# First batch of a cross-attention and MoE kernel: its transposes, its statistics, and the order of the weights around it

## The chip, the cores and the metric

The kernel runs on one core of a Trainium2 chip, as one program. The metric is the time of one execution on the device in microseconds (us), median of several runs.

## The reference, cut to what matters

Four batches of 512 rows by 512 columns in float32 pass through two blocks.

```
# block 1, cross-attention that mixes columns            x: [4, 512, 512]
ln     = layernorm(x)                                     # eps 1e-5
query  = ctx @ Wq.T + bq ; key = ctx @ Wk.T + bk          # ctx [4,512,256] -> [4,512,128]
att    = softmax(query @ key.T)                           # [512, 512] of each batch
x1     = x + ln @ att.T

# block 2, transformer layer on h = layernorm(x1); result is x1 + block2(h)
a      = rmsnorm(h, ln1_w)
q,k,v  = a @ wq, a @ wk, a @ wv                           # 16 heads of 128, causal softmax
h      = h + attention(q, k, v) @ wo
m      = rmsnorm(h, ln2_w)
out    = h + (6 best of 16 experts, I = 352, weighted)(m) + shared_expert(m)   # SI = 704
```

## The kernel before, in words

**Precision.** Every float32 operand of a product is kept as two float16 tiles, a high and a low half. `split` makes them: ACT writes the high half (line 73, scaled and rounded), DVE the low half (line 74, the scaled source less the high half). `mm3` (lines 80 to 88) does every product in three passes: high by high (L83), high by low (L86) and low by high (L87).

**Transposes.** `flip` (L90) is a DMA transpose that SP issues. It turns the softmax of block 1 (`pn` into `ptp`), the normalised rows of block 1 (`hh` into `hT`) and the softmax of every attention head (`pn` into `pt`).

**Order.** The instructions of each engine are put in order by a scheduler from the order in which the program issues them, and `after(ins, first)` (L93) adds a dependence for the order alone. The dictionary `zz` holds the instructions that later ones are tied to. Weights are staged through tiles of the pool `stg`, which has two buffers.

**Block 1 of a batch** is the generator `xattn(b)` (from L203). It yields between small steps, and `step(b, n)` (L371) advances it by n of them. Its steps are:

- load of the context, its split into `ctp`, the products `xq` that make query and key (L275 to 287), and for batch 0 the split of the loaded x transposed into `lnp` (`turn`, L268: high half on ACT, low half on GpSimd, L273). One yield.
- four times, for 128 rows of the attention: the product `en` (L306), maximum on DVE, exponential on ACT, reciprocal, split into `pn`, transpose into `ptp`. Batch 0 yields once for each of these, the others twice.
- the statistics of x (`stats`, L249: four times `bn_stats` and `bn_aggr` on DVE, a power on GpSimd, and `nb` on DVE) and the centring of x by `nb` (`center`, L265, four instructions on GpSimd). Batch 0 does them behind its last softmax, the others between softmax steps.
- four times, for 128 rows of x: the product `xm` of 12 passes (L335), the residual on DVE, a DMA of the sum to `x1_d`, mean and variance on DVE, a power on GpSimd that makes `r2` (L346), `hu` on DVE, `hd` on GpSimd (L353, the value that the second block adds to), the split into `hh` (L360) and the transpose into `hT`. Three yields each.

Batch 0 is run whole (`step(0, 99)`, L375). Behind it come the load of `ln2b`, two zero rows that GpSimd writes, the gate's weights and their split. Then batch 1 is advanced by nine steps (L389), which are all of its energies. What is left of batch 1, twelve steps, is given out two at a time (L809) behind each of the first six heads. The main loop does the four heads of the first two groups of weights for batch 0 alone, and then each further group, which is two heads, for batch 0 and behind it for batch 1. So the first head of batch 1 is the seventh head of the main loop; before that head `step(b, 99)` (L762) finishes the batch.

**The main loop** (from L756) goes over heads. A head is `queries` (L613: two products of 512 columns by 12 passes, for the very first head in two halves of 256 columns), `values` for a new group (L599, in two halves), `project` of a group that is ready (L671), `scores` (L630: product, mask and maximum on DVE, exponential on ACT, split, transpose), and `attend` of the head before (L658). For the first head the first half of the values comes ahead of the first half of the queries, and these are the first uses of `hT`.

`fetch` (L406) brings a head's weights: for a first use a load by SP into a staging tile, `split` into the tile that the products read, and a DMA of both halves to a scratch in memory, from which later batches load. The first head's `wqk0` and `wv0` are loaded ahead of all that and split behind the last softmax step of batch 0 (`zz["calm"]`) and behind `nb`. The load of `wqk1` is tied to the last transpose of batch 0.

`warm` (L185) issues TensorE products whose results nobody uses: 10 at the start, 8 behind the first `xq`, 22 behind the last `en` of batch 0.

Of the kernel before, what the change touches and what calls it, by code (L numbers as in the profile page):

```python
# [17 lines left out]
P = 128  # L18
# [37 lines left out]
def xattn_moe_block_kernel(ctx: ExitStack, tc: tile.TileContext, x, xT, ctxT, wqkx, bqk, ln1, ln2,  # L56
# [18 lines left out]

    def split1(hi, lo, src, eng=nc.vector):
        return (nc.scalar.activation(hi, src, AF.Copy),
                eng.tensor_tensor(lo, src, hi, ALU.subtract))
# [11 lines left out]
    def flip(o, i):  # L90
        return nc.sync.dma_start_transpose(out=o, in_=i)

# [98 lines left out]

    warm(10)
# [10 lines left out]
    def xattn(b):  # L203
# [7 lines left out]
        if b == 0:  # L211
            xT32 = [turned(j) for j in range(2)]
        xt = (ap_ if b else x2p).tile([P, NT, D], F32, tag="xt" if b else "x2", name=f"xt{b}")
        nc.sync.dma_start(xt, x[b].rearrange("(t p) d -> p t d", p=P))
        if b == 0:
            nc.sync.dma_start(ln1b, ln1.partition_broadcast(P))
# [5 lines left out]
        for j, ins in enumerate(split(ctp[:, 0], ctp[:, 1], ct32, HS)):  # L222
            if b == 1:
                after(ins, zz["calm"][j])
# [24 lines left out]
        def stats():  # L249
            mv = asm.tile([P, NT, 2], F32, name="mvs", bufs=2)  # L250
            for m in range(NT):
                st = asm.tile([P, 6], F32, name="st")
                ins = nc.vector.bn_stats(st, xt[:, m, :])
                if b < 2:
                    after(ins, zz["hh", 0] if b else zz["sm", 0][1])
                nc.vector.bn_aggr(mv[:, m, :], st)
            ins = nc.vector.tensor_scalar(rs, mv[:, :, 1], 1e-5, PS * PS, ALU.add, ALU.mult)
            if b == 0:
                zz["calm"] = zz["sm", 0][0], ins
            nc.gpsimd.tensor_tensor(rs, rs, mhalf, ALU.pow)  # L260
            ins = nc.vector.scalar_tensor_tensor(nb, mv[:, :, 0], -PS, rs, ALU.mult, ALU.mult)
            if b == 0:
                zz["nb"] = ins

        def center(t):  # L265
            nc.gpsimd.tensor_scalar(xt[:, t, :], xt[:, t, :], nb[:, t:t + 1], None, ALU.add)
# [28 lines left out]
        for m in range(NT):  # L295
# [24 lines left out]
            zz["ptp", b] = flip(ptp[:, :, ml], pn)  # L320
            yield
        if b == 0:
            stats()
            after(nc.vector.tensor_scalar(ln1b, ln1b, HS, None, ALU.mult), zz["calm"][1])
            for t in range(NT):
                center(t)
            warm(22, last)
        if b < 2:
            x2s[b] = x2p.tile([P, NT, D], F32, tag="x2", name="x2")
        hT[b] = hpool.tile([P, 2 * C, S], F16, tag="hT", name=f"hT{b}")  # L330
        for t in range(NT):
            ps = bank("w", f"xm{b}_{t}")
            tl = slice(t * P, (t + 1) * P)
            xv = xt[:, t, :]
            zz["xm", b, t] = mm3(ps, [(lnp[:, c, tl], lnp[:, C + c, tl], ptp[:, c], ptp[:, C + c]) for c in range(C)])  # L335
            nc.vector.scalar_tensor_tensor(xv, ps, rs[:, t:t + 1], xv, ALU.mult, ALU.add)
# [23 lines left out]
            zz["hh", b] = split(hi, lo, hu, r2[:, 1:2])[1]  # L360
            zz["hT", b] = flip(hT[b][:, :, tl], hh)
# [13 lines left out]
    step(0, 99)  # L375
    ln2b = const.tile([P, D], F32, name="ln2b")
    nc.sync.dma_start(ln2b, ln2.partition_broadcast(P))
    after(nc.vector.tensor_scalar(ln2b, ln2b, HS, None, ALU.mult), zz["calm"][1])
    zrow = xp.tile([1, D], F32, tag="x1t", name="zrow", bufs=1)
# [885 lines left out]
```

## Time and profile before

| | |
|---|---|
| five runs, us | 1810.59, 1797.95, 1794.96, 1805.03, 1801.44 |
| their median, us | 1801.44 |
| the profiled execution, us | 1799.48 |
| its span, us | 1797.8 |
| mean granted TensorE clock | 0.983 |
| TensorE busy, us (share of the span) | 1727.1 (96%) |
| DVE busy, us | 1115.4 (62%) |
| ACT busy, us | 829.1 (46%) |
| GpSimd busy, us | 465.9 (26%) |

The profile is of one execution. Its span runs from the first to the last recorded instruction. PE is TensorE's products, PEld its weight loads, DVE is VectorE, ACT is ScalarE, POOL is GpSimd, and SP is the engine that issues most DMAs. Times are microseconds from the start of the span. In a row of the timeline come the start, the duration, the engine, the line of the program, the operation, the tiles written and read, their sizes, and in brackets how long the engine had waited and for whom. In a table of stages, each engine's busy time stands with the number of its instructions, and behind them the mean granted clock of TensorE (1.00 is full), the mean busy share of the 16 DMA engines and the GB/s that they moved.

### The profile page before, as it was taken

The numbers are of one execution on the slowest core, as the hardware profiler recorded it, in microseconds if no ns is written. First come the engines' busy times: TensorE is split into PE (matmuls) and PEld (weight loads), VectorE is DVE, ScalarE is ACT, GpSimd is POOL, SyncE is SP. The second block draws the span as 40 slices with busy tenths as digits, with TensorE's granted clock in tenths as the row PEclk, the third lists the DMA queues.
The fourth block names the chain that finished last, engine by engine and source line by source line (L and its number), as shares of the span: only waits on it lengthen the run. The fifth ranks groups of instructions, "written<-read, shape, count | busy, mean of one in ns | idle before, by whom it ended". The sixth has DMA issues, their size and how long they took to land. (4 is left out here: it accounts for less than half of the span.)

```text
span 1797.8 us, 27676 instructions
## 1 busy us (share of the span) xinstructions
PE 1727.1 (96%) x9919; PEld 933.9 (52%) x9919; DVE 1115.4 (62%) x2766; ACT 829.1 (46%) x1711; POOL 465.9 (26%) x576
## 2 busy tenths in 40 slices
PE   8899999999998999999999799999999999999998
PEld 3454555555554555556556344355555555555553
DVE  6786777777784677676667343744444444456755
ACT  4555655455543545554445322334444444444421
POOL 5423111130256252121113625300000000025653
PEclk9999999999998999999999899999999999999999
DMA  7876868475576776555457533755545545679766
GB/s 240 207 182 175 213 146 191 109 194 119 136 180 196 155 183 163 128 112 115 111 118 147 171 68 126 225 155 147 149 147 178 140 146 142 185 206 259 228 194 206
DMA packets 392724, 296.24 MB, mean 165 GB/s; under 512 B 334880, under 2 KB 335136, under 8 KB 391808
## 3 DMA queue, kind: packets, MB, share of 16 engines
q1 hardware_dynamic: 359456, 180.32, 42.6%
q0 software_dynamic: 33120, 114.06, 19.6%
q8 instruction: 80, 1.31, 0.3%
q14 instruction: 68, 0.56, 0.1%
HBM read 124.81 MB, written 88.94 MB: 119 GB/s over the span
## 5 line engine op out<-in xcount | busy, mean ns | idle before, releaser
L1140 POOL DMA_INDIRECT yg<-y_d,yrc x96 | 111.2, 1159 | 523.2 <-DVE hf L1043 441.1
L649 ACT ACTIVATE pe<-pe,bnm 128x128 f32<-128x128 f32 (+3 forms) x256 | 142.4, 557 | 161.9 <-DVE bnm L647 159.6
L83 PE MATMUL qk<-hT,wqk 128*128 128x512 f16 (+1 forms) x520 | 196.1, 377 | 6.3 <-DMA hT<-hh 6.3
L87 PE MATMUL qk<-hT,wqk 128*128 128x512 f16 (+1 forms) x520 | 196.0, 377 | 0.0
L86 PE MATMUL qk<-hT,wqk 128*128 128x512 f16 (+1 forms) x520 | 196.0, 377 | 0.0
L74 DVE SCALAR_TENSOR_TENSOR pn<-pe,brc,pn 128x128 f16<-128x128 f32 (+3 forms) x256 | 146.1, 581 | 22.4 <-ACT pn L73 16.9
L647 DVE CUSTOM_DVE_ANT_0 pe<-sc,causal 128x128 f32<-128x128 f32 (+3 forms) x256 | 117.2, 486 | 62.2 <-PE sc L644 54.8
L73 ACT ACTIVATE pn<-pe,brc 128x128 f16<-128x128 f32 (+3 forms) x256 | 133.7, 553 | 26.4 <-ACT pe L649 16.8
L86 PE MATMUL v<-wv,hT 128*128 128x256 f16 x512 | 140.4, 274 | 2.5 <-issue 2.4
L87 PE MATMUL v<-wv,hT 128*128 128x256 f16 x512 | 140.6, 275 | 1.8 <-issue 1.8
L83 PE MATMUL v<-wv,hT 128*128 128x256 f16 x512 | 140.2, 274 | 1.5 <-DMA hT<-hh 0.8
L83 PE MATMUL g<-xT,wt 128*128 128x384 f16 (+2 forms) x384 | 127.3, 331 | 0.0
L86 PE MATMUL g<-xT,wt 128*128 128x384 f16 (+2 forms) x384 | 127.2, 331 | 0.0
L87 PE MATMUL g<-xT,wt 128*128 128x384 f16 (+2 forms) x384 | 127.2, 331 | 0.0
L1029 ACT ACTIVATE hT_e<-hf 128x384 f16<-128x384 f32 (+3 forms) x96 | 51.0, 532 | 141.9 <-DVE hf L1043 133.7
L681 DVE SCALAR_TENSOR_TENSOR x<-wo,x 128x512 f32<-128x512 f32 x128 | 87.5, 687 | 37.2 <-PE wo L87 36.9
L83 PE MATMUL y<-dt,hT_e 128*128 128x512 f16 (+1 forms) x288 | 109.4, 380 | 0.0
L87 PE MATMUL y<-dt,hT_e 128*128 128x512 f16 (+1 forms) x288 | 108.9, 378 | 0.0
L86 PE MATMUL y<-dt,hT_e 128*128 128x512 f16 (+1 forms) x288 | 108.9, 378 | 0.0
L73 ACT ACTIVATE qkt<-qk 128x512 f16<-128x512 f32 x128 | 74.6, 586 | 71.9 <-PE qk L87 70.5
L463 POOL DMA_INDIRECT xs_d<-h2p,slotu x96 | 96.5, 1005 | 27.6 <-issue 27.5
L74 DVE SCALAR_TENSOR_TENSOR qkt<-qk,qkt 128x512 f16<-128x512 f32 x128 | 87.6, 687 | 21.7 <-ACT qkt L73 17.9
(323 smaller groups left out, 4034.9 us busy)
## 6 DMA issues: line engine op xcount, KB each, us to landing
y_d<-yt SPq DMA_DIRECT2D x96, 256.0 KB
est<-in_ew_dram SPq DMA_DIRECT2D x32, 704.0 KB
est<-in_ed_dram SPq DMA_DIRECT2D x16, 768.0 KB
wqk<-wqk_d POOLq DMA_DIRECT2D x20, 512.0 KB
wqk_st<-in_wqk_dram SPq DMA_DIRECT2D x16, 512.0 KB
wqk_d<-wqk POOLq DMA_DIRECT2D x15, 512.0 KB
xs_d<-causal POOLq DMA_DIRECT2D x16, 384.0 KB
wv<-wv_d POOLq DMA_DIRECT2D x10, 512.0 KB
```

The lines of the kernel that those rows point to most:

```text
L73: return (nc.scalar.activation(hi, src, AF.Copy, scale=scale), nc.vector.scalar_tensor_tensor(lo, src, scale, hi, ALU.mult, ALU.subtract))
L74: nc.vector.scalar_tensor_tensor(lo, src, scale, hi, ALU.mult, ALU.subtract))
L83: ins = nc.tensor.matmul(o, lh, rh, start=start and j == 0, stop=False)
L86: nc.tensor.matmul(o, lh, rl, start=False, stop=False)
L87: ins = nc.tensor.matmul(o, ll, rh, start=False, stop=stop and j == n - 1)
L463: ins = nc.gpsimd.indirect_dma_start(out=xs_d, out_offset=bass.IndirectOffsetOnAxis(ap=slotu[:, tt, k:k + 1], axis=0), in_=h2ps[tt], in_of ...
L647: nc.vector.tensor_tensor_reduce(pe, ps[:, :w], causal[:, S - w:], -1.0, 3e38, ALU.add, ALU.min, nm)
L649: nc.scalar.activation(pe, pe, AF.Exp, bias=nm, scale=-1.0, accum_out=sm)
L681: nc.vector.scalar_tensor_tensor(x2[:, t, :], ps, 1.0 / (VS * WS), x2[:, t, :], ALU.mult, ALU.add)
L1029: nc.scalar.activation(hT[:R, ic, :w], hf, AF.Copy)
L1140: nc.gpsimd.indirect_dma_start(out=yg, out_offset=None, in_=src, in_offset=bass.IndirectOffsetOnAxis(ap=idx[:, tt, k:k + 1], axis=0))
```

## The change

The program computes the same. For batch 0 of block 1 it differs in these points; batches 1 to 3 keep the DMA transposes and the statistics where they were.

- `swap` replaces `flip` for `ptp` and `hT` of batch 0: for each half, four products with an identity matrix in float16 (`id16`) put the transposed blocks into a PSUM bank, and a copy brings them to SBUF. The high halves' copies are on ACT, the low halves' on DVE (`ptp`), or all on ACT (`hT`).
- x of batch 0 is loaded ahead of its transposed form, which now follows behind it on SP.
- The statistics of batch 0 are tied behind the third of the four transposes. Its centring is on ACT instead of GpSimd.
- The last run of `warm` has 12 products instead of 22.
- `xm` of batch 0 is done in pieces: the first two row blocks by 128 columns, in the order in which `ptp` comes, the last two whole, in the banks of the tag `s`. The residual of the last two is tied behind the second `hh`.
- Batch 0 is advanced by 11 steps, which are its first two row blocks. Its remaining steps, and what stood behind them, are now in `second_half`, which is called in the first head between the first and the second halves of values and queries. `second_half` then advances batch 1 by five steps; the main loop by four instead of two behind each of the first six heads.
- `wqk1` is fetched ahead of `second_half`, and held for the second head.
- In the first six heads, `fetch` uses `split_in_place` instead of `split`: ACT writes the high half and then scales the staged weights in place, and GpSimd subtracts.

```diff
@@ -73,6 +73,13 @@
         return (nc.scalar.activation(hi, src, AF.Copy, scale=scale),
                 nc.vector.scalar_tensor_tensor(lo, src, scale, hi, ALU.mult, ALU.subtract))
 
+    def split_in_place(hi, lo, src, scale):
+        ins = nc.scalar.activation(hi, src, AF.Copy, scale=scale)
+        more = nc.scalar.activation(src, src, AF.Copy, scale=scale)
+        if "center" in zz:
+            after(more, zz["center"])
+        return ins, nc.gpsimd.tensor_tensor(lo, src, hi, ALU.subtract)
+
     def split1(hi, lo, src, eng=nc.vector):
         return (nc.scalar.activation(hi, src, AF.Copy),
                 eng.tensor_tensor(lo, src, hi, ALU.subtract))
@@ -89,6 +96,16 @@
 
     def flip(o, i):
         return nc.sync.dma_start_transpose(out=o, in_=i)
+
+    def swap(o, i, tag, low):
+        done = []
+        for a, put in enumerate((nc.scalar.copy, low)):
+            ps = bank(tag, "swap")
+            for c in range(C):
+                j = (a * C + c) * P
+                nc.tensor.matmul(ps[:, c * P:(c + 1) * P], i[:, j:j + P], id16, start=True, stop=True)
+            done.append(put(o[:, a * C:(a + 1) * C, :], ps.rearrange("p (c q) -> p c q", c=C)))
+        return done
 
     def after(ins, first):
         tc.add_manual_dep(ins.ins, first.ins.name,
@@ -189,6 +206,8 @@
             if first:
                 after(ins, first)
 
+    id16 = ap_.tile([P, P], F16, name="id16")
+    nc.vector.tensor_copy(id16, ident)
     warm(10)
     ct0 = ctx_load(0)
     wx32 = at_.tile([P, 2 * CC * P], F32, tag="f", name="wx32")
@@ -208,11 +227,10 @@
             nc.sync.dma_start(t, xT[b, j])
             return t
 
-        if b == 0:
-            xT32 = [turned(j) for j in range(2)]
         xt = (ap_ if b else x2p).tile([P, NT, D], F32, tag="xt" if b else "x2", name=f"xt{b}")
         nc.sync.dma_start(xt, x[b].rearrange("(t p) d -> p t d", p=P))
         if b == 0:
+            xT32 = [turned(j) for j in range(2)]
             nc.sync.dma_start(ln1b, ln1.partition_broadcast(P))
             for nm, src in (("wqk0", wqk[0]), ("wv0", wv[0])):
                 t = vp.tile([P, NT, 2, GW], F16, tag="vt", name=f"{nm}_st")
@@ -221,7 +239,7 @@
         ctp = ap_.tile([P, 2, CC, S], F16, tag="lnp", name="ctp")
         for j, ins in enumerate(split(ctp[:, 0], ctp[:, 1], ct32, HS)):
             if b == 1:
-                after(ins, zz["calm"][j])
+                after(ins, zz["hh", 0] if j else zz["hi", 0])
         spare = dict(pm=[(he, "pe3"), (xp, "h2"), (he, "pe3"), (xp, "x1t")],
                      pn=[(hq, "qk0"), (hq, "qk1"), (he, "pn3"), (rp, "h2p")], hh=[(he, "pn3"), (rp, "h2p")])
         spare.update(hu=spare["pm"], qf=spare["pm"])
@@ -252,17 +270,17 @@
                 st = asm.tile([P, 6], F32, name="st")
                 ins = nc.vector.bn_stats(st, xt[:, m, :])
                 if b < 2:
-                    after(ins, zz["hh", 0] if b else zz["sm", 0][1])
+                    after(ins, zz["hh", 0] if b else zz["third"])
                 nc.vector.bn_aggr(mv[:, m, :], st)
             ins = nc.vector.tensor_scalar(rs, mv[:, :, 1], 1e-5, PS * PS, ALU.add, ALU.mult)
+            nc.gpsimd.tensor_tensor(rs, rs, mhalf, ALU.pow)
+            zz["nb"] = nc.vector.scalar_tensor_tensor(nb, mv[:, :, 0], -PS, rs, ALU.mult, ALU.mult)
+
+        def center(t):
             if b == 0:
-                zz["calm"] = zz["sm", 0][0], ins
-            nc.gpsimd.tensor_tensor(rs, rs, mhalf, ALU.pow)
-            ins = nc.vector.scalar_tensor_tensor(nb, mv[:, :, 0], -PS, rs, ALU.mult, ALU.mult)
-            if b == 0:
-                zz["nb"] = ins
-
-        def center(t):
+                zz["center"] = nc.scalar.activation(xt[:, t, :], xt[:, t, :], AF.Identity, bias=nb[:, t:t + 1])
+                after(zz["center"], zz["calm"][0])
+                return
             nc.gpsimd.tensor_scalar(xt[:, t, :], xt[:, t, :], nb[:, t:t + 1], None, ALU.add)
 
         def turn(j, t):
@@ -317,23 +335,43 @@
             nc.vector.tensor_scalar(rc, rc, PS, None, ALU.mult)
             pn, hi, lo = pair(tmp("pn", F16))
             zz["sm", b] = split(hi, lo, pm, rc)
-            zz["ptp", b] = flip(ptp[:, :, ml], pn)
+            if b:
+                flip(ptp[:, :, ml], pn)
+            else:
+                zz["third"] = zz["calm"][1] if m else None
+                zz["calm"] = swap(ptp[:, :, ml], pn, "a", nc.vector.tensor_copy)
             yield
         if b == 0:
+            after(nc.vector.tensor_scalar(ln1b, ln1b, HS, None, ALU.mult), zz["calm"][1])
             stats()
-            after(nc.vector.tensor_scalar(ln1b, ln1b, HS, None, ALU.mult), zz["calm"][1])
             for t in range(NT):
                 center(t)
-            warm(22, last)
+            warm(12, last)
         if b < 2:
             x2s[b] = x2p.tile([P, NT, D], F32, tag="x2", name="x2")
         hT[b] = hpool.tile([P, 2 * C, S], F16, tag="hT", name=f"hT{b}")
+        def product(t, tag):
+            ps = bank(tag, f"xm{b}_{t}")
+            tl = slice(t * P, (t + 1) * P)
+            zz["xm", b, t] = mm3(ps, [(lnp[:, c, tl], lnp[:, C + c, tl], ptp[:, c], ptp[:, C + c]) for c in range(C)])
+            return ps
+
+        early_xm = [bank("w", f"xm{b}_{t}") for t in range(0 if b else 2)]
+        for m in range(NT):
+            ml = slice(m * P, (m + 1) * P)
+            for t, ps in enumerate(early_xm):
+                tl = slice(t * P, (t + 1) * P)
+                zz["xm", b, t] = mm3(ps[:, ml], [(lnp[:, c, tl], lnp[:, C + c, tl], ptp[:, c, ml], ptp[:, C + c, ml])
+                                                 for c in range(C)])
+        if b == 0:
+            early_xm += [product(t, "s") for t in range(2, NT)]
         for t in range(NT):
-            ps = bank("w", f"xm{b}_{t}")
             tl = slice(t * P, (t + 1) * P)
             xv = xt[:, t, :]
-            zz["xm", b, t] = mm3(ps, [(lnp[:, c, tl], lnp[:, C + c, tl], ptp[:, c], ptp[:, C + c]) for c in range(C)])
-            nc.vector.scalar_tensor_tensor(xv, ps, rs[:, t:t + 1], xv, ALU.mult, ALU.add)
+            ps = product(t, "w") if b else early_xm[t]
+            ins = nc.vector.scalar_tensor_tensor(xv, ps, rs[:, t:t + 1], xv, ALU.mult, ALU.add)
+            if b == 0 and t >= 2:
+                after(ins, zz["hh", 0])
             q = nc.gpsimd if b else nc.sync
             q.dma_start(x1_d[b][:, t, :], xv)
             st = asm.tile([P, 6], F32, name="st")
@@ -357,8 +395,11 @@
                 nc.sync.dma_start(out[b, tl], hd)
             yield
             hh, hi, lo = pair(tmp("hh", F16))
-            zz["hh", b] = split(hi, lo, hu, r2[:, 1:2])[1]
-            zz["hT", b] = flip(hT[b][:, :, tl], hh)
+            zz["hi", b], zz["hh", b] = split(hi, lo, hu, r2[:, 1:2])
+            if b:
+                flip(hT[b][:, :, tl], hh)
+            else:
+                swap(hT[b][:, :, tl], hh, "as"[t // 2], nc.scalar.copy)
             yield
 
     if stop == "A":
@@ -372,21 +413,24 @@
         for _ in range(n):
             next(bg[b], None)
 
-    step(0, 99)
+    step(0, 5 + 6)
     ln2b = const.tile([P, D], F32, name="ln2b")
-    nc.sync.dma_start(ln2b, ln2.partition_broadcast(P))
-    after(nc.vector.tensor_scalar(ln2b, ln2b, HS, None, ALU.mult), zz["calm"][1])
-    zrow = xp.tile([1, D], F32, tag="x1t", name="zrow", bufs=1)
-    nc.vector.memset(zrow, 0.0)
-    nc.gpsimd.dma_start(y_d[0:1, :], zrow)
-    nc.gpsimd.dma_start(yo_d[0:1, :], zrow)
     g32 = const.tile([P, C * E], F32, name="g32")
-    nc.sync.dma_start(g32, gate)
     gtp = const.tile([P, 2, C, E], F16, name="gtp")
     gtf = gtp.rearrange("p a c e -> p a (c e)")
-    for j, ins in enumerate(split(gtf[:, 0], gtf[:, 1], g32, WS)):
-        after(ins, zz["calm"][j])
-    step(1, 1 + 2 * NT)
+
+    def second_half():
+        step(0, 99)
+        nc.sync.dma_start(ln2b, ln2.partition_broadcast(P))
+        after(nc.vector.tensor_scalar(ln2b, ln2b, HS, None, ALU.mult), zz["hh", 0])
+        zrow = xp.tile([1, D], F32, tag="x1t", name="zrow", bufs=1)
+        nc.vector.memset(zrow, 0.0)
+        nc.gpsimd.dma_start(y_d[0:1, :], zrow)
+        nc.gpsimd.dma_start(yo_d[0:1, :], zrow)
+        nc.sync.dma_start(g32, gate)
+        for j, ins in enumerate(split(gtf[:, 0], gtf[:, 1], g32, WS)):
+            after(ins, zz["hh", 0] if j else zz["hi", 0])
+        step(1, 5)
 
     shx = {}
 
@@ -402,6 +446,7 @@
             pieces.append((sdw[:, :, j:j + 1024], sd[:, j:j + 1024]))
 
     held, partner, seen = {}, {}, set()
+    low_on_pool = [True]
 
     def fetch(b, g, pool, tag, n, src, scr, nm):
         if held.get(nm, (None,))[0] == (b, g):
@@ -418,17 +463,14 @@
             st_ = early_st[nm]
         else:
             st_ = stg.tile([P, 1024], F32, tag="st", name=f"{nm}_st")
-            ins = nc.sync.dma_start(st_[:, :n], src)
-            if nm == "wqk1":
-                after(ins, zz["hT", 0])
-        for j, ins in enumerate(split(w[:, 0], w[:, 1], st_[:, :n], WS)):
-            if first:
-                after(ins, zz["nb"] if j else zz["calm"][0])
+            nc.sync.dma_start(st_[:, :n], src)
+        cut = split_in_place if low_on_pool[0] else split
+        for j, ins in enumerate(cut(w[:, 0], w[:, 1], st_[:, :n], WS)):
+            if j == 0 and (first or nm == "wqk1"):
+                after(ins, zz["calm"][0] if first else zz["center"])
         ins = (nc.sync if nm == "wqk0" else nc.gpsimd).dma_start(scr, w.rearrange("p a n -> p (a n)"))
         if nm != "wqk0":
             zz["pad"] = ins
-        if nm == "wqk0":
-            after(ins, zz["ptp", 0])
         return w
 
     pieces = []
@@ -754,11 +796,13 @@
     ready = []
     bring = iter([j for j in range(2, B) for _ in range(5 * NT + 1)])
     for n in range(NH + LAG + 1):
+        low_on_pool[0] = n < 6
         if n < NH:
             b, h = heads[n]
             if b not in opened:
                 opened.add(b)
-                step(b, 99)
+                if n:
+                    step(b, 99)
                 if b == B - 1:
                     shared_pool()
             parts = [queries(b, h)]
@@ -768,6 +812,8 @@
                 parts.reverse()
                 for p in parts:
                     next(p)
+                held["wqk1"] = (0, 0), fetch(0, 0, wp, "wqk", 1024, wqk[1], wqk_d[1], "wqk1")
+                second_half()
             for p in parts:
                 for _ in p:
                     pass
@@ -806,7 +852,7 @@
         if H // 2 <= n < H // 2 + E:
             pad_rows(n - H // 2)
         if n < 6:
-            step(1, 2)
+            step(1, 4)
         else:
             for _, j in zip(range(2 - n % 2), bring):
                 step(j)
```

## The prediction

> **What bounds the kernel now.** I read the page first, then the stages of the opening, then TensorE's waits, then single rows of the timeline.
>
> The page:
> ```profile
> span 1797.8 us, 27676 instructions
> ...
> PE 1727.1 (96%) x9919; PEld 933.9 (52%) x9919; DVE 1115.4 (62%) x2766; ACT 829.1 (46%) x1711; POOL 465.9 (26%) x576
> ```
> TensorE is busy 96% of the span. A change that leaves its products alone can only shorten the time in which it does not stream. The changed program's order of products is the old one again, row for row, from about a quarter of the kernel on, so what counts is how much is lost before that.
>
> The stages up to 200 us (PE, PEld, DVE, ACT, POOL busy, then clock, DMA share, GB/s):
> ```profile
> 0.00:41.11 41.11, 32.14 (x124) 12.76 (x124) 28.57 (x71) 18.77 (x31) 20.36 (x23) 0.92 0.80 254
> 41.11:51.75 10.64, 7.36 (x58) 5.51 (x58) 8.86 (x17) 4.17 (x6) 9.15 (x6) 1.00 0.40 87
> 51.75:77.97 26.22, 20.62 (x136) 13.08 (x137) 18.46 (x45) 15.70 (x31) 11.16 (x12) 0.99 0.88 207
> 77.97:145.12 67.15, 62.88 (x359) 34.16 (x359) 57.57 (x167) 39.37 (x89) 12.80 (x17) 0.98 0.85 212
> ```
> TensorE's waits in the first 200 us, and the rows that end them:
> ```profile
> PE qk L83 <- DMA hT<-hh: 6.3, 2, 3.3
> PE sc L642 <- DVE bnm L647: 5.6, 1, 5.6
> PE xm L83 <- DMA ptp<-pn: 5.6, 1, 5.6
> ```
> ```profile
> 51.75 0.28 PE L83 MATMUL qk<-hT,wqk 128*128 128x256 f16 x1 [3.28 <-DMA hT<-hh]
> ...
> 73.52 0.72 ACT L73 ACTIVATE pn<-pm,rc 128x512 f16<-128x512 f32 x1 [4.78 <-DMA ptp<-pn]
> ...
> 77.97 0.37 PE L642 MATMUL sc<-qkt,qkt 128*128 128x256 f16 x1 [5.61 <-DVE bnm L647]
> ...
> 145.12 0.39 PE L83 MATMUL qk<-hT,wqk 128*128 128x512 f16 x1 [3.03 <-DMA hT<-hh]
> ```
> The stall before 77.97 goes back through DVE and ACT to a DMA transpose of batch 1. At 145.12 the first product of batch 1's heads waits for batch 1's last transpose. I take that product as the meeting point: before it both programs do the same products.
>
> **The yardstick.** From 57.65 to 60.67 fourteen products of 512 columns start, 0.2157 us each: one unit. Ahead of the meeting point lie xq 24, en 24, xm 96, six heads' queries 144, three groups' values 72, scores 45, five heads' av 37.5, two wo 48: 490.5 units, 105.8 us. Before loses 145.1 - 105.8 = 39.3 us, and 1.7 more in the half-clock window (3.41 us) after the stall: 41.0. On the way, at 41.11, 84 units (18.1) are done: 23.0 lost; at 51.75, 26.3; the third stall adds 5.6 and a half-clock window 1.7, the fourth 3.0, crumbs 2.7.
>
> **The change, part by part.**
>
> *TensorE transposes, first batch.* Eight DMA transposes go (SP issue 1.24 to 2.79 us each). 64 products of 128 columns come, 0.055 us apart in the score rows: 3.5 us, in gaps where TensorE waits anyway (uncovered, they would cost 3.5). Sixteen evictions come; no row has them, the nearest are the 0.58 (ACT) and 0.68 us (DVE) of the vt halves. The last softmax halves end at 18.15 (ACT) and 19.04 (DVE) as before. With three banks and two copies squeezed between, DVE's third copy ends near 21.5; the four moved statistics (2.47 us) stand ahead of the fourth in DVE's queue, which ends near 24.6. Before, the last transpose landed at 25.1: 0.5 us won.
>
> *Statistics, centring.* After 24.6: ln1b 0.42, aggregates 0.36, rs 0.17, GpSimd's power 1.16, nb 0.15, then centring on ACT 0.7: the first residual runs at 27.7 (30.24 before; centring left GpSimd, where four took 8.16 us). Two residuals and statistics at DVE's row prices give the first r2 at 30.9.
>
> *Low halves on GpSimd.* Its row for the same form, 2.13 us, replaces DVE's 1.22; ACT pays an in-place scaling, 1.05, for each. Eleven weights: DVE -13, GpSimd +23, ACT +12 us. Here it bites: ACT scales wv only behind four centrings, at 30.4. GpSimd's queue is then wv low (to 32.6), power (0.75, 33.3), wqk low (35.5), power (36.2). hh follows 0.72 on ACT, 0.74 on DVE, then transposes: the first v product at 38.0. With collisions on the SBUF port:
> ```profile
> 44.63 2.13 POOL L273 TENSOR_TENSOR lnp<-xT,lnp 128x1024 f16<-128x1024 f32 x1
> 44.69 2.08 DVE L351 SCALAR_TENSOR_TENSOR nb<-mv,r 128x1 f32<-128x1 f32 x1 [1.25 <-POOL r L346]
> ```
> a 0.15 us instruction took 2.08, until GpSimd's was done. Two of the hu and hh steps could each lose a us: 40.0. I take 38.5, for most small DVE steps beside GpSimd's earlier 2.13 us rows (13.90 on) kept their 0.15. By then 72 units are done (15.5 us; batch 1's xq is no longer there): 23.0 lost, as before.
>
> The Trainium skill, SBUF — State Buffer, section "SBUF: two separate sides", says that a DVE instruction with two SBUF inputs and a GpSimd instruction lock each other out for a whole instruction, which speaks against this part. By that rule the start would be 40.0 and the final sum 1.5 us later.
>
> *Second half of batch 0.* GpSimd after 36.2: a DMA issue (0.8), the second head's low half (39.1), two hd (0.76 and 1.78), an issue (0.6), third power 43.0; hh, residual and statistics again, fourth power near 47.5; hh, then ACT has batch 1's ctp (1.05) ahead of two copies: queries' second half at 50.3, against 51.75. But TensorE then has only v and q to do: 20.7 us done, 29.6 lost, 3.3 more than before, because xq and en of batch 1 (4.5 us) filled that gap. Idle through a whole clock window, it restarts at half clock: about 1.6, 31.2 lost.
>
> *Second head's weights early, third's late.* The order on SP puts the third head's load behind staging that GpSimd frees: power, four centrings (1.57 each), one low half of xT, 65.2 us. Load 3.9 (50.17 to 54.03), hi 1.05, an exp 0.7, scaling 1.05, low 2.13: 74. TensorE gets there near 71.7 to 72.5: 0 to 4 us, I take 1.5. The fourth head's load stands on SP ahead of three transposes for the first attend and waits for that low half: they issue from 74.3, the last lands near 80 if it takes 3.1 as at 37.92. TensorE arrives near 77.7: I take 2.4; with the row at 65.69, whose transpose landed after 13.5 us, it is 12.
>
> *Batch 1 in steps of four.* Its last xm moves ahead of the fifth head: the 3.0 us wait and 1.7 of half clock at 145 go. DVE, 57.57 of 67.15 us busy, is relieved: crumbs 1.7 for 2.7. xt's load ahead of xT moves xT back by xt's 2.8 us, to 11.1; ACT reads it at 11.6: nothing, but with 0.5 us to spare (beyond, ACT's softmax slips with it). Ten fewer warm-up products lie in idle time.
>
> *Sum.* 31.2 + 1.5 + 2.4 + 1.7 = 36.8 against 41.0: 4.2 us less. The profiled execution took 1799.5 us (span 1797.8 and 1.7 around it): 1795.3. The median of the five runs is 2.0 above it, so I forecast 1797.
>
> A rule on the clock bears on the attend stall. These stretches of one clock window show TensorE's busy time, clock and DMA:
> ```profile
> 1012.64:1016.05 3.41, 1.39 (x5) 1.00 0.95 278
> 1016.05:1019.46 3.41, 0.94 (x2) 0.50 0.37 151
> 186.61:190.02 3.41, 1.72 (x15) 1.00 0.77 240
> 190.02:193.43 3.41, 3.21 (x17) 1.00 0.91 287
> ```
> A window 1.39 busy was followed by half clock, one 1.72 busy was not. So a stall of 1.9 us can cost 1.7 more, and I keep that for the range. The skill's TensorE: Matmul & The Clock Gate, section "What's actually happening", asks for an idle window of about 3.4 us; by it the stall of 2.4 costs nothing further. The row differs, and it decides.
>
> **The rivals.** (About 0.5%, 9 us, is what a measurement of this kernel can tell from no change.)
>
> *Within 0.5%, forecast, 0.44.* Earlier start and a later wait nearly cancel.
>
> *Faster, 0.35.* GpSimd and SP keep up: start at 38.0, second half at 49 with 28.3 lost, no half clock, neither weight nor attend waits, crumbs 1.7: 30.0 lost, 11 us won, 1790. For it: the DMAs are spread out and eight transposes fewer are in the way. Against it: GpSimd's 2.13 us rows stand in one queue with the powers.
>
> *Slower, 0.21.* SP's order becomes the bound. If the first attend's last transpose takes 13.5 us as at 65.69, the wait is 12.7 instead of 2.4; with one half-clock window (1.7) and the xm transposes behind (1.3), 13 more: 1810. It decides from 13 us in flight on. For it: DMA share 0.88 at that place; against: the loads are now paced.
>
> The unknowns' ends give 1790 and 1810; the five runs lie 6.5 below and 9.2 above their median, and a median of runs moves by about half of that at most: 1783 to 1812. Faster 0.35, same 0.44, slower 0.21.
>
> **What would show it.** Right: no DMA transpose of ptp or hT for batch 0; first v product near 38.5, TensorE idle some 7 us before queries near 50; waits of 1 to 3 us before the third head's queries and the first av; no wait at batch 1's first queries; losses up to there near 37 us. Wrong: GpSimd's low half well off 2.1 us; v later than 40; an av wait over 10; a wait at the meeting point still; or the later three quarters of the kernel changing by more than a few us, which none of these steps explains.

## The result and the profile after

The changed kernel takes 1812.66 us (median of 44 runs), the kernel before 1808.12 (median of 86): ratio 1.0024, interval [1.0013, 1.0036], 4.3 us slower. The forecast, 1797, was 4.4 us below the median of the five runs that it started from, and that median lies 6.7 us below the one of all 86. The profiled execution took 1807.8 us.

The page, then the stages up to the point where the 105.8 us of products ahead of batch 1's first head are done (151.2; columns as before):

```profile
span 1806.1 us, 27928 instructions
...
PE 1730.2 (96%) x10045; PEld 941.1 (52%) x10045; DVE 1113.2 (62%) x2760; ACT 848.8 (47%) x1738; POOL 475.9 (26%) x583
```
```profile
0.00:41.12 41.12, 29.78 (x223) 16.65 (x224) 28.20 (x63) 26.09 (x40) 16.57 (x20) 0.92 0.54 199
41.12:51.78 10.66, 8.71 (x68) 6.62 (x66) 7.68 (x19) 5.22 (x10) 5.28 (x7) 0.82 0.47 148
51.78:84.75 32.97, 26.58 (x146) 14.27 (x144) 24.17 (x74) 25.31 (x53) 17.03 (x12) 0.95 0.46 121
84.75:151.20 66.45, 64.05 (x367) 35.44 (x368) 51.01 (x135) 38.92 (x75) 29.63 (x30) 0.97 0.90 225
```

The first v product starts at 41.12, where it started before (41.11). The 3.0 us wait at batch 1's first head is gone, the 5.6 us wait too. In their place, in TensorE's waits of the first 200 us, stand the transposes of hh, the scores and the first av (in each row: us in total, how many waits, the longest):

```profile
PE swap L106 <- ACT hh L73: 6.5, 3, 3.6
PE sc L684 <- ACT qkt L73: 4.0, 2, 2.1
PE av L90 <- DMA pt<-pn: 3.4, 1, 3.4
PE sc L684 <- DVE bnm L689: 2.3, 2, 2.0
...
PE sc L685 <- DVE qkt L74: 1.2, 1, 1.2
...
PE sc L684 <- ACT pm L332: 1.0, 2, 0.8
```

By the forecast's yardstick (time at which n us of products are done, less n; warm-up and transposes not counted), at 120 us of products, just behind the meeting point, the changed kernel has lost 45.3 us and the one before 41.1. At 200 us of products it is 53.2 against 45.4. These two marks (lost at 120 and at 200 us of products) and the start of the first v product ("first v") are given for every kernel below, each from its one profile.

### The profile page after: what moved, and what is told of

Same layout as the page of the kernel before. It is cut to its first block, busy times and chain, and to the rows that moved or that the text cites. A ratio compares the mean times of both kernels' runs of the same rounds, so it can differ in the third digit from the quotient of the medians.

```text
span 1806.1 us, 27928 instructions
## 1 busy us (share of the span) xinstructions
PE 1730.2 (96%) x10045; PEld 941.1 (52%) x10045; DVE 1113.2 (62%) x2760; ACT 848.8 (47%) x1738; POOL 475.9 (26%) x583
## 3 DMA queue, kind: packets, MB, share of 16 engines
q0 software_dynamic: 33120, 114.06, 19.2%
## 4 chain that ended last, share of the span: by engine, by line
PE 64%; DMA 6%; issue 5%; DVE 5%; ACT 1%; POOL 1%; another core or an unknown queue 1%; SPq 0%; POOLq 0%; ACTq 0%; DVEq 0%
PE qk L93 4%; PE qk L94 4%; PE qk L90 4%; PE g L93 3%; PE g L90 3%; PE g L94 3%; PE y L90 3%; PE y L93 3%; PE y L94 3%; DMA yg<-y_d,yrc 3%; PE wo L93 2%; PE wo L94 2%; PE wo L90 2%; PE u L90 2%; PE u L94 2%
## 5 line engine op out<-in xcount | busy, mean ns | idle before, releaser
L1186 POOL DMA_INDIRECT yg<-y_d,yrc x96 | 106.6, 1110 | 530.5 <-PE u L94 439.7
```

What stands on the lines that cost most here:

```text
L1186: nc.gpsimd.indirect_dma_start(out=yg, out_offset=None, in_=src, in_offset=bass.IndirectOffsetOnAxis(ap=idx[:, tt, k:k + 1], axis=0))
```

## The experiments

Three parts of the change could be undone alone. F: the low halves of the first three weights (wv0, wqk0, wqk1). L: those of the later weights of the first six heads. X: batch 1's xq, which before filled the gap between batch 0's two halves. The experiments were run in five sessions. In the first two (e1 to e8) the kernel before takes 1771 to 1772 us, in the other three 1797 to 1807. Ratios are to the kernel before in the same session, from 8 to 12 runs of each changed program. What separates the two kinds of session is not known: chip number 4 of the record gave 1771 us in one session and 1799 in a later one.

**Low halves on DVE.**
```diff
-        cut = split_in_place if low_on_pool[0] else split
+        cut = split
```


> The changed kernel with the low halves of all early weights on DVE again (split in place of split_in_place), nothing else changed. Theory A (GpSimd's low halves and ACT's extra scalings are what came out dearer than forecast): hu and nb of the first rows take 0.74 and 0.16 us again instead of 2.65 and 2.08, the first v product comes near 38.9 instead of 41.1, the staging tiles come free some 2 us earlier, so the wait before the first av falls from 3.4 to under 1 us without a half-clock window behind it; lost up to the first head of batch 1 about 38 instead of 45.4 us, time about 6 us below the changed kernel, ratio to before 0.999. Rival B (batch 1's energies, now among the first heads' scores, overfill DVE and ACT between 62 and 86 us, and DVE gets 1.22 us more for each weight): the start gains 2 us, the waits from 70 to 118 us stay or grow, time within 2 us of the changed kernel. Rival C (the swaps' round trips set the start): v stays at 41.

Ratio 0.9992 [0.9965, 1.0019]. First v 38.72; lost 41.7 at the first mark, 45.5 at the second. The start came as theory A said, the time too; less of the middle came back than it said (41.7, not 38).

**Only the later ones on DVE (L).**
```diff
-        low_on_pool[0] = n < 6
+        low_on_pool[0] = n == 0
```


> The changed kernel with GpSimd's low halves kept for the first head's weights and the second head's, and DVE's split for all later ones. The start must stay at 41.1 in every theory. Theory A: waits between 68 and 118 us fall by about 4 us (third head's weights 0.8, av 3.4 and its half clock 1.7, the wait at 116.8), time 4 us below the changed kernel. Rival B: these waits stay within 1 us of what they are, time the same as the changed kernel.

Ratio 0.9978 [0.9953, 1.0004], by the ratios 8 to 10 us below the changed kernel (1.0024, and 1.0037 in e5). First v 40.97. The waits of scores between 55 and 205 us fell from 8.5 us to 1.5, but in this profile a DMA transpose for xm (4.5) and av (3.5) took their place: lost 46.0 and 52.9. So by the yardstick theory A's waits did not fall here, though the time did.

**DMA transposes again.** `swap` replaced by `flip` in both places.

> The changed kernel with the DMA transposes back for ptp and hT of batch 0. The second hh low half ended at 40.65 and the first v product started at 41.12, 0.5 us later; before it was 38.5 and 41.1, 2.6 later. Theory A: ptp's swaps hide behind the centring (the first residual waited for it at 28.2), hT's save about 2.1 us, so the first v product comes near 43.2 and the second half's queries 2 us later too; time 2 to 5 us above the changed kernel. Rival C (the swaps themselves cost the time): v at 41 or earlier, time as before the change or below.

Ratio 1.0036 [1.0007, 1.0065], lost 45.8 and 52.1. First v at 41.55, 0.4 us later than with TensorE's transposes and not 2.1. The edit moves more than the transposes: the statistics are tied to the softmax again, so nb comes at 24.01 (27.27), GpSimd's three low halves end at 34.89, ahead of the second hu and of hh (nb of the first row took 0.15 us, not 2.08), and the first residual waits for TensorE's xm until 30.05 (28.23). In this version what the transposes save at the start is small.

**Batch 1 as before.**
```diff
-        step(1, 5)
+        step(1, 9)
-            step(1, 4)
+            step(1, 2)
```


> The changed kernel with batch 1 advanced as before: nine steps (all its energies) at once after the second half of batch 0, then two behind each head. Theory B: the energies stand together ahead of the first heads' scores again, the waits at 70 to 77 us move into one wait, and the wait at the first head of batch 1 (3.0 us and a half-clock window of 1.7) is back; lost up to there 45 to 50 us, time 0 to 4 us above the changed kernel. If spreading batch 1 over the first heads is what cost the time, it is 3 us or more below the changed kernel instead.

Ratio 1.0064 [1.0038, 1.0090], lost 50.2 and 55.5. Spreading batch 1 is not what cost the time.

**The changed kernel again.**

> The changed kernel itself once more, as a control beside the other three on this chip. Ratio to before 1.001 to 1.004. The losses up to the first head of batch 1 (45.4 us) come again within 1.5 us, if they are the program's order; the 5 us that its first profile lost between 183 and 200 us (ACT waiting for weights, the scores' operands behind it) come again if that is the order too, and are gone if it was one execution's DMA.

Ratio 1.0037 [1.0012, 1.0062]; first v 40.47, lost 44.6 and 55.8. So the loss behind the meeting point belongs to the program too.

**The transposes alone, in the kernel before.**

> The kernel before with one part of the change alone: batch 0's ptp and hT are transposed by TensorE, all else as it was (statistics, GpSimd's centring, DVE's low halves, batch 1 at once). The first xm product comes before 23 us instead of 25.2, but the powers still wait behind GpSimd's centring until 33.0, so hh stays and only the last step, hh to v, shortens from 2.6 to about 0.8 us: first v product near 39.3, second queries' half near 50.2. Theory A: time 1 to 3 us below before (ratio 0.9985). Rival C (swaps cost more than they save): ratio above 1.001.

Ratio 1.0009 [0.9979, 1.0038]: no difference to be seen. First v 42.81, later and not earlier; lost 38.6 and 45.3.

**The low halves alone, in the kernel before.**

> The kernel before with another part of the change alone: GpSimd makes the low halves of the early weights, ACT scales them in place. Theory A (this part is dear by itself): the two low halves stand ahead of the four centrings on GpSimd, the first power slips from 33.0 to about 37, the first v product from 41.1 to about 44.5, and DVE's small steps beside GpSimd take 2 us each; ratio to before 1.002 to 1.0045. Rival B (the low halves are cheap, the spreading of batch 1 is what costs): ratio within 0.001 of 1.

Ratio 1.0004 [0.9976, 1.0032]. First v 45.69 and lost 45.0 and 51.7, but no time: a miss for theory A. GpSimd's low halves are not dear in every program.

**Low halves on DVE, in order.**
```diff
+            zz["rs"] = ins
...
-            after(nc.vector.tensor_scalar(ln1b, ln1b, HS, None, ALU.mult), zz["calm"][1])
             stats()
+            after(nc.vector.tensor_scalar(ln1b, ln1b, HS, None, ALU.mult), zz["rs"])
...
-        cut = split_in_place if low_on_pool[0] else split
+        cut = split
...
+            elif nm in ("wv0", "wqk0", "wqk1"):
+                after(ins, zz["rs"] if nm == "wv0" else zz["hh", 0])
```


> The changed kernel with all low halves on DVE (as in the first experiment), and three steps put behind others in DVE's queue: the first low half of wv and the scaling of ln1b behind rs, the low halves of wqk0 and wqk1 behind the second hh. In the first experiment they stood ahead: two lows (2.4 us) and ln1b (0.4) ahead of rs, one (1.2) ahead of hh. Theory A: rs 2.4 us earlier, second hh 2.5 to 3.5 earlier, first v product near 36.2 instead of 38.7, time 2 to 3 us below the first experiment, ratio to before near 0.998. If the time does not follow the start, what is won at the start is given back in the waits behind it.

Ratio 0.9951 [0.9928, 0.9974], faster than both kernels. First v 35.38, lost 39.6 and 44.6.

**Weight loads on GpSimd**, from the fourth head's on.
```diff
-            nc.sync.dma_start(st_[:, :n], src)
+            (nc.sync if nm in ("wqk1", "wqk2") else nc.gpsimd).dma_start(st_[:, :n], src)
```


> The changed kernel with the first loads of the weights, from the fourth head's on, issued by GpSimd instead of SP, so that on SP no load stands ahead of or behind a transpose. In the two profiles of the changed kernel ACT waited 7 us for a wqk load that SP issued at 179 behind four transposes, and the scores' operands behind it came late: 8 to 11 us were lost between the first head of batch 1 and 200 us, 4.3 before. Theory D (SP's order made that loss): it falls to 5 or less, time 3 to 6 us below the changed kernel, ratio to before 0.999 to 1.001. If the wait before the first av (3.4 us) comes from the fourth head's load ahead of its transposes on SP, it goes too; theory B (softmax of batch 1 and scores crowd DVE and ACT, so pn itself is late): it stays within 1 us. If neither loss falls, SP's order is not the cause.

Ratio 1.0018 [0.9991, 1.0044], not told apart from the changed kernel. Between the marks 2.0 us were lost instead of 8 to 11, as theory D said; the time that it forecast did not come. And av waited 7.2 us (3.4), and the first mark stands at 46.7.

**xq in the gap**, in the version of e8.
```diff
+                step(1, 1)
                 held["wqk1"] = (0, 0), fetch(0, 0, wp, "wqk", 1024, wqk[1], wqk_d[1], "wqk1")
...
-        step(1, 5)
+        step(1, 4)
...
-            if b == 0:
-                after(ins, zz["qf"])
+            if b < 2:
+                after(ins, zz["cp"] if b else zz["qf"])
```
(`zz["cp"]` is the last hT copy of batch 0.)

> The last version (low halves on DVE, three steps put behind others) with batch 1's xq ahead of batch 0's second half again, where it stood in the kernel before, and batch 1's xT splits behind batch 0's last hT copy. In that version TensorE lost 8.4 us between 16 and 21 units done, waiting for the second half of hT with nothing else to do. xq is 24 units, 5.2 us. Theory: 3 to 5 us of that gap is filled; first v product near 35.4 as there; the second half comes up to 2 us later for the ctp split and four evictions among its steps; time 1 to 4 us below that version, ratio to before 0.993 to 0.995. Against it: if the stretch behind is bound by DVE and ACT (theory B), the filled gap is lost again in the waits from 65 to 90 us and the ratio stays at 0.995.

Ratio 0.9917 [0.9883, 0.9951], lost only 30.5 and 35.9.

**Second head's weights late**: the line that fetches wqk1 ahead of `second_half` taken out.

> The changed kernel without the early fetch of the second head's weights: they are fetched when the second head comes. The part costs an in-place scaling and a high half on ACT (2.1 us) ahead of the first hh, and GpSimd's 2.1 us low half ahead of hd. Theory A: without it the first hh comes 0.3 to 1 us earlier, the first v product near 40.3, but the second head's queries wait for their weights (load 3.9, halves 4.2 us behind the second half): 2 to 6 us lost there; time 0 to 5 us above the changed kernel. If the part was a loss, time is 2 us or more below it.

Ratio 1.0018 [0.9988, 1.0048]; first v 39.84, the second head waited 5.5 us for its weights, lost 50.0 and 55.5. The time does not tell it from the changed kernel.

**The kernel before again**, one run.

> The kernel before once more, for a second profile on this chip. The losses up to the first head of batch 1 (41.1 us) and between it and 200 us (4.3) come again within 2 us if they belong to the program; the stretch behind 200 us shows how much one profile differs from another (76.6 us lost there in the first, 40 to 50 in the experiments' profiles).

1796.62 us, lost 38.9 and 44.3, so the marks repeat within 2.2 us.

**xq alone** (X): the edit of e10 in the changed kernel.

> The changed kernel with one thing undone: batch 1's xq stands ahead of batch 0's second half again (and batch 1's xT splits behind batch 0's last hT copy). GpSimd's low halves stay. Theory E (the moved xq is the main cause: TensorE has nothing to do between the halves, and batch 1's softmax starts late, among the first scores): first v product still near 41, lost between 16 and 26 units 3 instead of 6.4, between 26 and 120 units 7 to 9 instead of 12.5; time 6 to 10 us below the changed kernel, ratio to before near 0.998. Theory A (GpSimd's low halves are the main cause): the loss up to 120 units stays within 3 us of 45, ratio 1.001 or more.

Ratio 1.0042 [1.0012, 1.0073], lost 43.2 and 46.8. Theory E fell: by itself this wins no time.

**Two edits of e10's kernel**: the later low halves back on GpSimd, and (e15) the loads on GpSimd as in e9.

> The fast version (low halves on DVE, three steps put behind others, xq in the gap) with GpSimd's low halves and ACT's scalings brought back for the weights from the third head's on. The start stays at 35. Theory A: the waits between 26 and 120 units grow from 6 to 10 us or more, ratio to before 0.995 or above. Theory E: they stay within 2 us, ratio 0.991 to 0.993.

Ratio 1.0019 [0.9990, 1.0047], lost 38.1 and 44.5: as theory A said, and by more.

> The fast version with the first loads of the weights, from the fourth head's on, issued by GpSimd instead of SP. In the changed kernel this took the loss between 120 and 154 units from 8 to 11 down to 1.8, and the waits before the av products grew by 4 us ahead of that. The fast version loses 5.2 there. Theory D: 2 to 3 us less there, the same up to 120 units, ratio 0.990 to 0.991; if the av waits grow as they did, ratio 0.992 to 0.994.

Ratio 1.0013 [0.9980, 1.0046], lost 36.1 and 42.9. Loads on GpSimd lose about what that version won (0.9917, and 0.9969 when run again).

**The missing combinations** of F, L and X.

> The fast version (F, L and X) once more, beside the two missing combinations. Ratio to before 0.990 to 0.995; lost up to the first head of batch 1 within 3 us of 30.5. If it comes out above 0.996, its first result was chance.

> The changed kernel with the later weights' low halves on DVE (L) and xq back in the gap (X); the first three weights' low halves stay on GpSimd. Theory A (L is the large term): ratio 0.996 to 0.999, first v product still near 41. If X helps once L is mended, it is below the 0.9978 that L alone gave; if X gives nothing by itself, it is the same.

> The changed kernel with the low halves of the first three weights on DVE and in order (F), all others on GpSimd, xq where the change put it. First v product near 35.4. Theory A: F is worth 2 to 5 us against the changed kernel, ratio 1.000 to 1.002, because L is still to be paid. If the start's 5.7 us came through whole, ratio 0.9995 or less.

e16 gave 0.9969 [0.9937, 1.0002], e17 0.9986 [0.9959, 1.0013], e18 1.0021 [0.9991, 1.0052]. By the bound set for it (0.996), e16 says that the first 0.9917 of the same program was in part chance. All eight combinations together (F here is DVE and in order; the last column sums TensorE's waits of the score lines from 55 to 205 us):

| undone | ratio | first v | lost at 120 | lost at 200 | score waits |
|---|---|---|---|---|---|
| none | 1.0024, 1.0037 | 41.12, 40.47 | 45.3, 44.6 | 53.2, 55.8 | 8.5, 7.8 |
| X | 1.0042 | 40.55 | 43.2 | 46.8 | 3.3 |
| F | 1.0021 | 35.79 | 45.0 | 52.9 | 8.2 |
| F, X | 1.0019 | 34.90 | 38.1 | 44.5 | 8.7 |
| L | 0.9978 | 40.97 | 46.0 | 52.9 | 1.5 |
| L, X | 0.9986 | 40.47 | 33.1 | 41.4 | 2.7 |
| F, L | 0.9951 | 35.38 | 39.6 | 44.6 | 1.6 |
| F, L, X | 0.9917, 0.9969 | 35.09, 34.88 | 30.5, 30.3 | 35.9, 38.4 | 2.6, 2.6 |

Pairs that differ in one part only, repeated kernels averaged (1.0026, where the ratio of 44 runs weighs more, and 0.9943): L gives -0.48, -0.56, -0.70 and -0.76%, on average -0.62%, 11 us. F gives -0.05, -0.23, -0.27 and -0.43%, on average -0.25%, 4 us. X gives +0.16, +0.08, -0.02 and -0.08%. One such difference is uncertain by about 0.4%, an average of four by about 0.2%. That is noise within a session; the two results of F, L, X lie 0.52% apart, so between sessions it is somewhat more. The rows L and F, L come from the sessions in which the kernel before takes 1771 us, the others from the slower ones, and the changed kernel has a ratio from each kind. L has the same sign in all four pairs, two of them within the slower kind. So L counts by itself, F barely, X not.

## Why the prediction was wrong

The likeliest case, no change that a measurement tells (within 0.5%), is what came, but not for the reason given, an earlier start and a later wait that nearly cancel: there was no earlier start. That much was luck, and the 4.2 us forecast within the case have the wrong sign. Of the 15.7 us between 1797 and 1812.66, 6.7 are the low median of the five runs and 9.0 the sum.

The step that failed is the price of GpSimd's later low halves. The forecast put the stretch behind the second half at 5.6 us (third head's weights 1.5, first av 2.4, crumbs 1.7), and it lost 12.9. With L undone the ratio is 0.9978, 4.0 us below before, which is about what was forecast; over four pairs L is worth 0.62%, 11 us. A smaller miss is the start, 2.6 us late. L takes back ACT's scalings, GpSimd's subtractions and the longer hold of the staging tiles together; which of the three costs the time was not tried.

Of the signs named ahead, two of "wrong" came: a first v product later than 40, and 2.5 to 6.9 us more lost between the two marks. The av wait stayed under 10 us, and no wait stood at batch 1's first queries. The range's ends, 1783 and 1812, do not follow from the numbers beside them: half of 6.5 and of 9.2 on 1790 and 1810 gives 1787 to 1815.

**The start.** Forecast 38.5, measured 41.12 and 40.47. Two terms were near: fourth ptp copy done at 25.3 (24.6), first residual at 28.23 (27.7). GpSimd's queue ran in the order worked out, 0.6 to 1.0 us late: wv's low half until 33.2, second power until 37.15. What was mis-sized is DVE beside it:
```profile
31.06 2.12 POOL L81 TENSOR_TENSOR wv<-wv_st,wv 128x1024 f16<-128x1024 f32 x1 [3.82 <-ACT wv_st L78]
31.08 2.65 DVE L386 SCALAR_TENSOR_TENSOR hu<-xt,mv,ln1b 128x512 f32<-128x512 f32 x1
...
34.27 2.23 POOL L81 TENSOR_TENSOR wqk<-wqk_st,wqk 128x1024 f16<-128x1024 f32 x1
...
34.44 2.08 DVE L389 SCALAR_TENSOR_TENSOR nb<-mv,r 128x1 f32<-128x1 f32 x1
...
41.12 0.42 PE L90 MATMUL v<-wv,hT 128*128 128x256 f16 x1
```
In each pair the DVE row starts just behind GpSimd's (0.02 and 0.17 us) and ends with or after it: hu took 2.65 us instead of 0.74, nb 2.08 instead of 0.16. An hh low half took 1.52 beside wqk1's. I had taken half of one such collision. The estimate by the Trainium skill's rule (SBUF — State Buffer, section "SBUF: two separate sides") was 40.0, nearer than my 38.5, and the rows agree with it. Without GpSimd's halves and with DVE's own put behind these steps, in e8:
```profile
30.88 0.74 DVE L387 SCALAR_TENSOR_TENSOR hu<-xt,mv,ln1b 128x512 f32<-128x512 f32 x1
...
31.66 0.74 DVE L387 SCALAR_TENSOR_TENSOR hu<-xt,mv,ln1b 128x512 f32<-128x512 f32 x1
...
35.38 0.42 PE L90 MATMUL v<-wv,hT 128*128 128x256 f16 x1
```

**Second half of batch 0.** Forecast 50.3 with 31.2 us lost; measured 51.78 with 32.4. This term held, the half-clock window with it:
```profile
47.97:51.38 3.41, 1.46 (x20) 1.08 (x18) 2.16 (x7) 2.91 (x6) 1.90 (x2) 1.00 0.01 2
51.38:54.79 3.41, 3.41 (x17) 2.06 (x16) 3.37 (x7) 0.83 (x2) 0.17 (x1) 0.50 0.00 0
```
TensorE was busy for 1.46 of a window's 3.41 us, and the next was at half clock. This stands between the rows that the forecast had, 1.39 (half followed) and 1.72 (not), and below the idle time that the skill's clock page asks for (TensorE: Matmul & The Clock Gate, section "What's actually happening"). The row decides. In all twenty profiles together the border is not sharp: windows of up to 1.93 us of busy time were followed by half clock (e9, from 556.08), and windows down to 1.40 were not (e12, from 248.52).

**From there to the meeting point.** Forecast 5.6 us: third head's weights 1.5, first av 2.4, crumbs 1.7. Measured 12.9 (45.3 less 32.4): 3.8 up to 40 us of products, where waits for the weights account for 0.8 and for the scores and energies for most of the rest; 5.5 around the first av, 3.35 of them a wait, 1.7 half clock; 3.6 behind it. That no wait would be left at batch 1's first head was right. But the two waits that went came back as many small ones. Of these I had none, because I had priced a low half by its own rows and by who waits for that weight. ACT and DVE work in a fixed order, and in these rows what stands behind a late weight waits with it:
```profile
109.89 0.52 SPq L466 DMA_DIRECT2D wo_st<-in_wo_dram  x1
...
115.22 1.06 ACT L77 ACTIVATE wo<-wo_st 128x1024 f16<-128x1024 f32 x1 [1.94 <-DMA wo_st<-in_wo_dram]
116.18 0.58 ACT L73 ACTIVATE qkt<-qk 128x512 f16<-128x512 f32 x1
...
116.81 0.54 PE L684 MATMUL sc<-qkt,qkt 128*128 128x128 f16 x3 [1.96 <-ACT qkt L73]
```
The high half of wo waited 1.94 us for its load, the scores' operand stood behind it, and TensorE 1.96 us for that. The load goes into the staging tile that wv held: GpSimd's low half of wv ended at 108.10, 5.5 us after wv's high half had started (102.59), and SP issued the load at 109.89, behind a transpose. The score waits of e18 and of e8, which differ in the later low halves alone, from 55 to 200 us (e18 first):
```profile
PE sc L688 <- DVE qkt L74: 2.8, 2, 1.7
PE sc L687 <- DVE bnm L692: 2.1, 2, 1.9
PE sc L687 <- ACT qkt L73: 2.1, 2, 1.3
...
PE sc L687 <- ACT pm L333: 1.2, 3, 0.8
```
```profile
PE sc L687 <- ACT qkt L73: 1.2, 1, 1.2
...
PE sc L687 <- DVE bnm L692: 0.2, 1, 0.2
...
PE sc L687 <- ACT pm L333: 0.2, 1, 0.2
```
8.2 us against 1.6. In the table three of the four combinations with GpSimd's later halves wait about 8 us, the four without 1.5 to 2.7. ACT's waits for weight loads between 55 and 200 us fall less: 26.0 us in the changed kernel and 22.6 in e18, 19.2 in e2 and 18.6 in e8.

By the yardstick, the whole stretch from 26 to 120 us of products lost this much with GpSimd's later halves and with L undone: 12.9 and 12.8 with nothing else undone, 13.9 and 3.9 with X, 15.4 and 9.7 with F, 13.9 and 6.2 with F and X. In three pairs of four 6 to 10 us of the missing term come back; in the first pair, the changed kernel and e2, none do, though e2 took less time. The kernel before, profiled twice, lost 14.6 and 11.8 here, so one such figure is uncertain by some 3 us.

That a longer hold of the two staging tiles (high half, scaling and GpSimd's low half, 4.2 us by their rows, against 2.3 with DVE) makes the loads late is argued from these rows; it was not tried by itself.

**Behind the meeting point** the forecast had no change. Between the two marks the kernel before loses 4.3 and 5.4 us, the changed one 7.9 and 11.2. At 183 us ACT had waited 7.5 us for a wqk load, issued on SP behind four transposes. With the loads on GpSimd (e9) this loss was 2.0 us; it was not shown that time follows.

**The rivals.** The slower one (SP's order, first av 12.7 us late) did not come; av waited 3.4. The faster one needed a start at 38.0.

**What stays open.** The marks and the times agree only in the rough. L is worth 11 us in time and 2 to 8 by the second mark; X 7 to 12 by that mark and nothing in time. Behind 200 us of products the profiles lose between some 68 and 88 us in the slower sessions whatever the kernel, a spread larger than what is to be explained. Nor is it settled why the low halves cost nothing that was measured in the kernel before (e7: 1.0004, within 0.28%) and 0.6% here.

## What to carry to other kernels

Price a step that is moved to another engine by all that stands behind it on every in-order queue that it touches, also where the engine it leaves is the busier one: an added scaling on ACT and a longer hold of a staging tile delayed operands of quite other products. When a forecast removes two large waits, ask which rows were hidden under them; here nearly the same sum came back in small ones. And where each part alone is within the noise, the combinations of three parts told which one counts, though single profiles pointed to another.

## What the runs showed of the hardware

The same changed program lost 76.8 us behind its first 200 us of products in one profile and 40.7 in another session (e5); 34.1 and 14.6 of that fell between 900 and 1100 us of products. The kernel before had medians from 1771 to 1808 us by session, so only ratios within a session were used.

A GpSimd row can be drawn out beside DVE rows too: in e1 two powers on GpSimd, beside two hu rows (0.74 us each) and a low half (1.22) on DVE, took 3.07 us together, where in the changed kernel the powers took 0.69 to 1.14 each. This is one case.
